# Constant products in TensorE's pauses, another split of the first list, and its tokens by pairs of groups, in a mixture-of-experts kernel on Trainium2

## The chip, the cores and the metric

The kernel runs on one core of a Trainium2 chip. The core has TensorE (matrix products, 128 by 128), VectorE and ScalarE (elementwise work), GpSimd (here constants and the issue of indirect transfers) and SyncE (issue of transfers). In the profile they are called PE (its weight loads PEld), DVE, ACT, POOL and SP. The metric is the device time of one execution in microseconds. TensorE and PSUM ([...]where products land) are what the other engines work for.

## The reference

Eight batches of 512 tokens with 512 features are scaled by a style of the batch, multiplied by one 512x512 matrix, normalised, biased and clipped (y). A router gives each of the 4096 tokens a softmax score for 8 experts. Each expert takes the 1024 tokens with its highest scores, runs a feed-forward layer of width 2048 on them, and adds its output, times the score, to the rows of those tokens.

```python
styles = cond @ (affine_w / sqrt(256)).T + affine_b
y = clip(einsum('blc,oc->blo', x * styles[:, None], weight) * dcoefs[:, None] + bias, -256, 256)
scores = softmax(y.reshape(4096, 512) @ Wr)            # 8 experts
G, idx = top_k(scores.T, 1024)                         # each expert picks its tokens
h = gelu(einsum('ekd,edh->ekh', y_tokens[idx], W1) + b1)
X = einsum('ekh,ehd->ekd', h, W2) + b2
out = x + zeros.at[idx].add(G[..., None] * X)
```

## The kernel before, in words

**Stage 1, the projection (lines 285 to 707).** Batch 0 is turned by TensorE (`turn_x0`) and multiplied by the whole matrix; batches 1 to 7 are turned by VectorE (`turn_x`) and multiplied in seven products of half-size blocks instead of eight (`unit`, with sums of blocks). `in_order` (line 366) makes each TensorE instruction that it is given follow the one given before; everything else is placed by a planner from its estimates of time. The first TensorE work is the style product, which waits for the first two transfers. Behind each batch come `score_products` and `score_softmax` (line 515): the maximum, exponentials, their sum and its reciprocal, then the scores `S` (8 per token), a copy `S0` of expert 0's score, `reps` (S0 repeated, to be turned into `R`), and `topc`, which counts for each of 64 thresholds how many of the batch's tokens reach it (an elementwise comparison `getop`, then a reduction). `store_scores` writes S behind the features in `y_dram`, where a token's row is 512 features and 8 scores.

**The first list (`route_first`, line 205).** The 1024th highest score of expert 0 is found bit by bit. `tot_top` sums the counts over partitions with a product by `ones` and fixes the top 6 bits; six rounds fix 4 bits each. In a round VectorE compares all scores with 16 candidates (`mark`, L226), TensorE adds the counts (`tot`, L229), VectorE chooses (L234, L237). Then the ranks of the chosen tokens come from two products (`rank0`, L245 and L247) and some twelve small VectorE operations: each token's place in the list, split into `lo` (place modulo 128) and `hi` (place divided by 128). In TensorE's gaps the planner puts the transposes (L703) that turn the rows of the last five batches, which ScalarE copies out and SP stores to `y_dram`.

**The list of token numbers (`indices`, line 810).** `oh` is a one-hot row of `lo` (128 columns for each of 32 token columns), `hot` one of `hi` (8 columns), `val` is `hot` times the partition number and times the column's first token. 32 small products `oh` by `val` add up to a 128x8 table of token numbers, `idx`. For expert 0 oh is made in four parts, and eight products follow each.

**Tokens (`gather`, `prepare`, lines 852 and 890).** GpSimd issues eight indirect transfers, 128 rows of `y_dram` each (groups 0 to 7). For expert 0 TensorE turns each group (L910), VectorE copies it out of PSUM (L912) into the four quarter tiles `xT[i, k]` (i: groups 0 to 3 or 4 to 7; k: half of the features), ScalarE copies out the gain (L907). When all have come, `left_sums` (L883 to L886) makes s1 to s4 on whole tiles. A transfer that copies x into out is issued by GpSimd behind the eighth gather. For the other experts the tokens take another way, through a second table in memory and VectorE's transposes.

**Stage 2, the experts.** For each expert and each half of the width there are four `hidden_unit`s and four `out_unit`s. A unit is seven block products p1, p2, p6, p7, p5, p3, p4, each two accumulating products of 128x128 by 512 (hidden). p1 and p2 need the tokens' quarters 11 and 12, p6 needs s2, p7 s3, p5 s1, p3 s4. p1, p6, p5 and p3 share the bank `a`, and ScalarE takes a snapshot (`snap`, L971) between them. `in_turns` lets the last two products of a unit overlap the next unit. The lists of the seven other experts (`route_others`, with `mark` at L736 on VectorE and `tot_b` at L726 on TensorE) are worked out during the first hidden units.

Of the kernel before, what the change touches and what calls it, by code (L numbers as in the profile page):

```python
# [11 lines left out]
F32 = mybir.dt.float32  # L12
# [13 lines left out]
def tile_modulated_expert_choice_ffn(  # L26
# [26 lines left out]
    GH = HALF // P  # L53
    GAIN = 1.0 / math.sqrt(W)
# [18 lines left out]

    ident = const.tile([P, P], F32, name="ident")
# [3 lines left out]
    ones = const.tile([P, P], BF16, name="ones")  # L78
    nc.gpsimd.memset(ones, 1.0)
# [22 lines left out]
    iota_hi = const.tile([P, KG], BF16, name="iota_hi")  # L102
    nc.gpsimd.iota(iota_hi, pattern=[[1, KG]], base=0, channel_multiplier=0,
# [15 lines left out]
    NR = (30 - TOP) // RB  # L119
    M = 1 << RB  # L120
# [84 lines left out]
    def route_first(p1c, reps, topc):  # L205
# [6 lines left out]
        for n in range(B):  # L212
            nc.tensor.matmul(tot, ones, topc[:, n, :], start=(n == 0), stop=(n == B - 1))
# [6 lines left out]
        for n in range(NR):  # L220
            cand = rt2.tile([P, 1], I32, tag="cand0", name=f"cand0_{n}")
            nc.vector.tensor_scalar(cand, owns[:, n : n + 1], thr[:, 0:1].bitcast(I32), None,
                                    op0=ALU.bitwise_or)
            mark = p1c.tile([P, ST_G, P], BF16, tag="mark0", name=f"mark0_{n}")
            cnt = rt2.tile([P, 1], F32, tag="cnt0", name=f"cnt0_{n}")
            nc.vector.tensor_scalar(mark, R, cand.bitcast(F32), None, op0=ALU.is_ge, op1=ALU.add,  # L226
                                    accum_out=cnt)
            ps = ps_small.tile([P, M], F32, tag="small", name=f"tot0_{n}")
            nc.tensor.matmul(ps, cnt.to_broadcast([P, P]), of, start=True, stop=True)  # L229
            cands = rt2.tile([P, M], I32, tag="cands0", name=f"cands0_{n}")  # L230
            nc.vector.tensor_scalar(cands, digits[:, n, :], thr[:, 0:1].bitcast(I32), None,
                                    op0=ALU.bitwise_or)
            ok = rt2.tile([P, M], F32, tag="ok0", name=f"ok0_{n}")
            nc.vector.scalar_tensor_tensor(ok, ps, float(K), cands.bitcast(F32),  # L234
                                           op0=ALU.is_ge, op1=ALU.mult)
            thr = rt2.tile([P, 1], F32, tag="thr0", name=f"thr0_{n}")
            nc.vector.tensor_reduce(thr, ok, AX.X, ALU.max)  # L237
# [7 lines left out]
        nc.tensor.matmul(ps[:, 0, :, :].rearrange("p a t -> p (a t)"), ones, flat,  # L245
                         start=True, stop=True)
        nc.tensor.matmul(ps[:, 1, :, :].rearrange("p a t -> p (a t)"), upper, flat,  # L247
                         start=True, stop=True)
# [23 lines left out]
        nc.vector.tensor_scalar(part, pos_i, P - 1, None, op0=ALU.bitwise_and)  # L272
# [3 lines left out]
        nc.vector.tensor_scalar(part2, pos_i, 7, None, op0=ALU.logical_shift_right)  # L276
# [13 lines left out]
    with tc.tile_pool(name="p1c", bufs=1) as p1c, tc.tile_pool(name="p1", bufs=2) as p1, \  # L290
# [72 lines left out]

        behind = {}

        def in_order(make, engine="PE"):

            if engine in behind:
                with tc.issue_after(behind[engine].ins):
                    behind[engine] = make()  # L370
            else:
                behind[engine] = make()
            return behind[engine]
# [141 lines left out]
        def score_softmax(b, ps):  # L515
# [15 lines left out]
            nc.vector.tensor_tensor(S[:, here, :], ex,  # L531
                                    sm.unsqueeze(2).to_broadcast([P, LT, E]), ALU.mult)
            nc.vector.tensor_copy(S0[:, here], S[:, here, 0])
# [3 lines left out]
            nc.vector.tensor_tensor(ge, S0[:, here].unsqueeze(1).to_broadcast([P, 1 << TOP, LT]),  # L537
                                    top.bitcast(F32).unsqueeze(2).to_broadcast([P, 1 << TOP, LT]),
                                    ALU.is_ge)
# [152 lines left out]
        score_softmax(B - 1, lg)  # L692
# [3 lines left out]
        places = {0: route_first(p1c, reps, topc)}  # L696
# [113 lines left out]
    def indices(e):  # L810
# [7 lines left out]
            iota_hi.unsqueeze(1).to_broadcast([P, NT, KG]), ALU.is_equal,  # L818
# [6 lines left out]

        parts = 1 if e else 4
        for n in range(parts):
            here = slice(n * NT // parts, (n + 1) * NT // parts)
            nc.vector.tensor_tensor(  # L829
                oh[:, here, :], lo[:, here].unsqueeze(2).to_broadcast([P, NT // parts, P]),  # L830
                iota_lo.unsqueeze(1).to_broadcast([P, NT // parts, P]), ALU.is_equal,
            )
# [7 lines left out]
        nc.vector.tensor_copy(idx[:, e, :], idx_f)  # L840

# [10 lines left out]
    def gather(e, i):  # L852

        z = gp.tile([P, GH * YW], F32, tag="xg", name=f"xg_{e}_{i}")
        if e:
            rows = dram.tile([HALF, YW], F32, name=f"rows_{e}_{i}")
            z = z[:, 0 : GH * D].rearrange("p (t c) -> p t c", c=P)
        else:  # L860
            z = z.rearrange("p (g w) -> p g w", w=YW)
        for j in range(GH):
            g = i * GH + j
            to = gp.tile([P, YW], F32, tag="row", name=f"row_{e}_{g}", bufs=4) if e else z[:, j, :]
            sent = nc.gpsimd.indirect_dma_start(
                out=to[:, :], out_offset=None, in_=y_dram[:, :],
                in_offset=bass.IndirectOffsetOnAxis(ap=idx[:, e, g : g + 1], axis=0),
            )
            if e:
                nc.sync.dma_start(rows[j * P : (j + 1) * P, :], to)  # L870
        if e:
            for q in range(4):
                nc.sync.dma_start(z[q * TB : (q + 1) * TB, :, :],
                                  rows[:, q * P : (q + 1) * P].rearrange("(t a) c -> a t c", a=TB))
            with nc.allow_non_contiguous_dma(reason="512 values"):
                nc.sync.dma_start(gains[e][:, i * GH : (i + 1) * GH],
                                  rows[:, D + e : D + e + 1].rearrange("(g p) o -> p (g o)", p=P))
        gathered[e, i] = z
        return sent
# [9 lines left out]

    def prepare(e):  # L890

        xT = {}
        for i in range(2):
            for k in range(2):
                xT[i, k] = fx.tile([P, 2, HALF], F32, tag=f"xT{i}{k}", name=f"xT{i}{k}_{e}")
        gain = gains.pop(e)
        ngain = fx.tile([P, KG], F32, tag="ngain", name=f"ngain_{e}")
        for i in range(2):
            xg = gathered.pop((e, i))
            for k in range(2):  # L900
                if e:
                    nc.vector.transpose(
                        xT[i, k].rearrange("p j (t b) -> p t j b", b=TB),
                        xg[:, :, 2 * k * TB : 2 * (k + 1) * TB].rearrange("p t (j a) -> p t j a", a=TB))
            for j in range(0 if e else GH):
                g = i * GH + j
                nc.scalar.copy(gain[:, g : g + 1], xg[:, j, D + e : D + e + 1])  # L907
                ps = ps_t.tile([P, DC, P], F32, tag="t", name=f"ps_xg{e}_{g}")
                for dc in range(DC):
                    nc.tensor.transpose(ps[:, dc, :], xg[:, j, dc * P : (dc + 1) * P], ident)  # L910
                for k in range(2):
                    nc.vector.tensor_copy(xT[i, k][:, :, j * P : (j + 1) * P],  # L912
                                          ps[:, 2 * k : 2 * k + 2, :])
        nc.vector.tensor_scalar_mul(ngain, gain, -1.0)
        s = {n: fx.tile([P, 2, HALF], F32, tag=f"x{n}", name=f"x{n}_{e}")
             for n in ("s1", "s2", "s3", "s4")}
        left_sums(xT[0, 0], xT[0, 1], xT[1, 0], xT[1, 1], s)
        s["11"], s["12"], s["22"] = xT[0, 0], xT[0, 1], xT[1, 1]
        tokens[e] = s, gain, ngain
# [35 lines left out]

    def hidden_unit(e, p, u, H):

        s, _, _ = tokens[e]
# [6 lines left out]
        def mm(ps, left, right, start):  # L965
            product(ps, [blk[right][:, k, u * P : (u + 1) * P] for k in range(2)],
                    [s[left][:, k, :] for k in range(2)], start)

# [5 lines left out]
        def p1():  # L974
            st["a"] = bank("a", name, 2)
            mm(st["a"], "11", (0, 0), True)
            st["s1"] = snap(1)

        def p2():
            st["b"] = bank("b", name, 1)  # L980
            mm(st["b"], "12", (1, 0), True)
# [27 lines left out]
        return [p1, p2, p6, p7, p5, p3, p4]  # L1009
# [88 lines left out]
    def fetch(e):  # L1098
# [3 lines left out]
        for i in range(2):  # L1102
            sent = gather(e, i)
        return sent
# [5 lines left out]

    with tc.issue_after(fetch(0).ins):
        nc.gpsimd.dma_start(out.rearrange("b l d -> b (l d)").rearrange("b (r w) -> (b r) w", r=16),
                            x.rearrange("b l d -> b (l d)").rearrange("b (r w) -> (b r) w", r=16))
    prepare(0)
    for e in range(E):
        b2_sb = fx.tile([P, D], F32, tag="b2", name=f"b2_{e}")
        nc.sync.dma_start(b2_sb, b2[e, :].partition_broadcast(P))
        for p in range(NP):
            nxt = (e, p + 1) if p + 1 < NP else (e + 1, 0)
            H = fx.tile([P, U, 2, KG * P], F32, tag="H", name=f"H_{e}_{p}")  # L1120
# [5 lines left out]
            in_turns([partial(hidden_unit, e, p, u, H) for u in range(U)], work)  # L1126
# [48 lines left out]
```

## Time and profile before

| what | value |
|---|---|
| median of three runs | 1750.04 us (1749.76 to 1750.58) |
| the profiled execution | 1749.67 us, span from first to last instruction 1747.9 us |
| TensorE busy | 1708.3 us, 98% |
| VectorE, ScalarE, GpSimd busy | 835.7, 478.3, 292.2 us |
| chain that ended last | TensorE 87%, VectorE 2% |
| mean granted clock of TensorE | 0.992 |

In the profile a line of an order of time gives start and duration in us, the engine, the line of the kernel, the operation, the tile written, the tiles read, the shape, the type and how many records, and in square brackets how long the engine was idle before and what ended that. An f32 product shows as two records, a transpose as one. A line of a table of stages gives the stage, its length, then busy us and instruction counts of PE, PEld, DVE, ACT and POOL, the granted clock of TensorE, the busy share of the DMA engines and GB/s. Times of a line come from the one profiled execution.

### The profile page before, as it was taken

Reading aid. Unit: us, or ns where it says so; the run is one execution under the profiler, and the core shown is the slowest. Engines: PE = TensorE matmul, PEld = TensorE weight load, DVE = VectorE, ACT = ScalarE, POOL = GpSimd, SP = SyncE. Lnnn points to the kernel's source line nnn. Section 1 sums busy time; section 2 is a strip of 40 time slices with the busy share of each in tenths; the row PEclk is TensorE's granted clock in tenths of the full one; section 3 lists DMA queues with packets and bytes.
Section 4 is the critical chain, followed back from the end, with each engine's and each line's share of the span. In section 5 each row is a group of like instructions: output and inputs, shape, how many; then the busy total and the mean of one; then the engine's idle time right before and its main releaser. Section 6 shows DMA issues by size and latency. Waiting matters only on the chain.

```text
span 1747.9 us, 17152 instructions
## 1 busy us (share of the span) xinstructions
PE 1708.3 (98%) x6522; PEld 1128.9 (65%) x6522; DVE 835.7 (48%) x1465; ACT 478.3 (27%) x842; POOL 292.2 (17%) x238
## 2 busy tenths in 40 slices
PE   8995999999999999999999999999999999999997
PEld 4774475665748485666748485766758484756656
DVE  5885883624536254524535254614445254614341
ACT  3543312223131322223231313222231313222231
POOL 0112013020222013020312013110312012110202
PEclk9997999999999999999999999999999999999999
DMA  9625627541573227441574237442574137332403
GB/s 205 172 50 177 211 49 165 121 90 48 96 201 67 54 52 173 109 84 50 98 197 79 48 64 179 89 80 55 108 184 88 45 66 182 79 79 61 84 0 49
DMA packets 143250, 178.57 MB, mean 102 GB/s; under 512 B 16824, under 2 KB 92856, under 8 KB 143040
## 3 DMA queue, kind: packets, MB, share of 16 engines
q1 hardware_dynamic: 118240, 115.19, 24.5%
q0 software_dynamic: 24912, 62.27, 21.1%
q8 instruction: 51, 0.84, 0.2%
q14 instruction: 31, 0.25, 0.1%
q10 hardware_dynamic: 16, 0.02, 0.0%
HBM read 120.46 MB, written 65.37 MB: 106 GB/s over the span
## 4 chain that ended last, share of the span: by engine, by line
PE 87%; DVE 2%; issue 0%; DMA 0%; POOLq 0%; POOL 0%; DVEq 0%
PE ps_a_o L953 25%; PE ps_a_h L953 25%; PE ps_c_o L953 12%; PE ps_c_h L953 12%; PE ps_b_h L953 6%; PE ps_b_o L953 6%; DVE mark L736 0%; PE ps_idx L835 0%; DVE oh L829 0%; DMA xg<-y_dram,idx 0%; PE ps_xg L910 0%; DVE ps_b_h L982 0%; POOLq L1171 0%; DVE hs_o L884 0%; DVE hs_o L883 0%
## 5 line engine op out<-in xcount | busy, mean ns | idle before, releaser
L1065 POOL DMA_INDIRECT out<-o_o,idx x128 | 212.3, 1659 | 1248.8 <-DVE o_o L1062 553.2
L953 PE MATMUL ps_a_o<-w_t,hs_o 128*128 128x256 f32 x1024 | 243.6, 380 | 1.2
L953 PE MATMUL ps_a_h<-xs,w_t 128*128 128x512 f32 x512 | 241.1, 593 | 0.0
L953 PEld LDWEIGHTS ps_a_o<-w_t,hs_o 128*128 128x128 f32 x1024 | 192.3, 190 | 33.4 <-issue 7.0
L971 ACT COPY snap_h<-ps_a_h 128x512 f32<-128x512 f32 x192 | 111.7, 582 | 236.9 <-PE ps_a_h L953 231.8
L953 PEld LDWEIGHTS ps_a_h<-xs,w_t 128*128 128x128 f32 x512 | 97.0, 190 | 123.0 <-issue 122.1
L1032 ACT ACTIVATE snap_o<-ps_a_o,gain 128x256 f32<-128x256 f32 x128 | 60.6, 474 | 347.5 <-PE ps_a_o L953 347.5
L997 DVE TENSOR_TENSOR snap_h<-snap_h,ps_c_h 128x512 f32<-128x512 f32 x64 | 43.9, 686 | 217.5 <-ACT snap_h L971 217.5
L982 DVE TENSOR_TENSOR ps_b_h<-ps_b_h,snap_h 128x512 f32<-128x512 f32 x64 | 44.7, 699 | 202.9 <-PE ps_b_h L953 202.9
L953 PE MATMUL ps_a_h<-xT,w 128*128 128x512 f32 x256 | 125.6, 598 | 0.0
L953 PE MATMUL ps_a_o<-w,H 128*128 128x256 f32 x512 | 124.1, 379 | 0.0
L953 PE MATMUL ps_c_o<-w,hs_o 128*128 128x256 f32 x512 | 123.8, 379 | 0.0
L953 PE MATMUL ps_a_h<-xs,w 128*128 128x512 f32 x256 | 122.0, 599 | 0.0
L953 PE MATMUL ps_a_o<-w,hs_o 128*128 128x256 f32 x512 | 121.5, 380 | 0.0
L953 PE MATMUL ps_b_o<-w,H 128*128 128x256 f32 x512 | 121.2, 379 | 0.0
L953 PE MATMUL ps_b_h<-xT,w 128*128 128x512 f32 x256 | 120.8, 593 | 0.0
L953 PE MATMUL ps_c_h<-xs,w 128*128 128x512 f32 x256 | 120.5, 593 | 0.0
L953 PE MATMUL ps_c_h<-xT,w_t 128*128 128x512 f32 x256 | 120.5, 593 | 0.0
L953 PE MATMUL ps_c_o<-w_t,H 128*128 128x256 f32 x504 | 119.1, 379 | 0.0
L953 PEld LDWEIGHTS ps_a_o<-w,H 128*128 128x128 f32 x512 | 97.1, 190 | 27.0 <-issue 15.5
L953 PEld LDWEIGHTS ps_a_o<-w,hs_o 128*128 128x128 f32 x512 | 96.0, 190 | 21.4 <-ACT snap_o L1032 8.9
L953 PEld LDWEIGHTS ps_c_o<-w,hs_o 128*128 128x128 f32 x512 | 97.1, 190 | 14.0 <-issue 0.6
(248 smaller groups left out, 1935.9 us busy)
## 6 DMA issues: line engine op xcount, KB each, us to landing
w<-in_w SPq DMA_DIRECT2D x120, 512.0 KB, 4.0
rows<-row SPq DMA_DIRECT2D x56, 260.0 KB, 4.0
xg<-rows SPq DMA_DIRECT2D x56, 256.0 KB, 6.6
x<-in_x SPq DMA_DIRECT2D x28, 256.0 KB, 8.8
y_dram<-ytok SPq DMA_DIRECT2D x5, 1024.0 KB, 4.4
w<-in_w SPq DMA_DIRECT2D x32, 128.0 KB, 4.1
y_dram<-ytok POOLq DMA_DIRECT2D x12, 256.0 KB, 4.8
b<-in_b SPq DMA_DIRECT2D x8, 256.0 KB, 4.0
```

The costliest lines, as they stand in the source:

```text
L953: nc.tensor.matmul(ps, lefts[k], rights[k], start=(start and k == 0), stop=(k == n - 1), skip_group_check=True)
L971: nc.scalar.copy(t, st["a"])
L982: added = nc.vector.tensor_add(st["b"], st["b"], st["s1"])
L997: nc.vector.tensor_add(st["u4"], st["u4"], st["c"])
L1032: nc.scalar.mul(t, st["a"], scale)
L1065: nc.gpsimd.indirect_dma_start(out=last_rows[g] if e == E - 1 else out_rows, out_offset=bass.IndirectOffsetOnAxis(ap=idx[:, e, g : g + 1], ...
```

## The change

`ones` is made first. `idle(n, ps)` issues n constant bf16 products of 128x128 by 512 (ones by ones) into a PSUM tile that nobody reads, each in order behind the TensorE instruction given to `in_order` before. There are nine at the very start, four after the count of each of the last two rounds, eight after the rank products, and sixteen after the products of the first list.

In the last batch S0 is made from the exponentials and the reciprocal directly, S comes after `getop`, and the reduction into `topc` is left out: `tot_top` adds the four slices of `getop` by four products.

The place in the first list is split into 64 low and 16 high values: `oh` has 64 columns, `hot` 16. One half of `val` is made by ScalarE. Each token column has two products, for the two halves of the partitions of the table. hot, val and oh lie in the two buffers that hold the gathered tokens afterwards.

The gathers come in pairs (group j of each half). After the transposes of a pair, VectorE copies the first half's group and ScalarE the second's, `left_sums` works on that pair's 128 columns, and units 0 and 1 multiply their p1 and p2 for these columns (`begin`); the second unit's bank b is taken from the ring of c. The gains are copied in two operations behind all tokens. For the other experts the code is moved, with the same instructions.

```diff
+    IDLE0, IDLE1, IDLE2 = 9, 8, 16
...
+    def idle(n, ps):
+        for _ in range(n):
+            in_order(partial(nc.tensor.matmul, ps.rearrange("p (a k) -> p a k", k=P), ones,
+                             ones.unsqueeze(1).to_broadcast([P, HALF // P, P]), start=True, stop=True))
+
+    ones = const.tile([P, P], BF16, name="ones")
+    nc.gpsimd.memset(ones, 1.0)
+    idle(IDLE0, ps_mm.tile([P, HALF], F32, tag="c", name="ps_idle0", bufs=2))
...
+    LO, HI = P // 2, 2 * KG
...
-        for n in range(B):
-            nc.tensor.matmul(tot, ones, topc[:, n, :], start=(n == 0), stop=(n == B - 1))
+        for n in range(B - 1):
+            nc.tensor.matmul(tot, ones, topc[:, n, :], start=(n == 0), stop=False)
+        for t in range(LT):
+            nc.tensor.matmul(tot, ones, last_top[:, :, t], start=False, stop=(t == LT - 1))
...
+            if n > NR - 3:
+                idle(4, ps_mm.tile([P, HALF], F32, tag="a", name=f"ps_idle_{n}", bufs=2))
...
+        idle(IDLE1, ps_mm.tile([P, HALF], F32, tag="b", name="ps_idle1"))
...
-        nc.vector.tensor_scalar(part, pos_i, P - 1, None, op0=ALU.bitwise_and)
+        nc.vector.tensor_scalar(part, pos_i, LO - 1, None, op0=ALU.bitwise_and)
...
-            nc.vector.tensor_tensor(S[:, here, :], ex,
-                                    sm.unsqueeze(2).to_broadcast([P, LT, E]), ALU.mult)
-            nc.vector.tensor_copy(S0[:, here], S[:, here, 0])
+            last = b == B - 1
+            if not last:
+                scores()
+            nc.vector.tensor_mul(S0[:, here], ex[:, :, 0], sm)
...
+            if last:
+                with tc.issue_after(done.ins):
+                    scores()
+                return ge
...
+    def first_indices():
+        lo, hi = places[0]
...
+        nc.vector.tensor_tensor(hot, hi.unsqueeze(2).to_broadcast([P, NT, HI]),
+                                iota_hi.unsqueeze(1).to_broadcast([P, NT, HI]), ALU.is_equal)
...
+        nc.scalar.mul(val[:, :, 0, :], hot, iota_p[:, 0:1])
+        nc.vector.tensor_tensor(val[:, :, 1, :], hot,
+                                iota_t.unsqueeze(2).to_broadcast([P, NT, HI]), ALU.mult)
+        parts = 4
+        ps = ps_small.tile([P, 2, KG], F32, tag="small", name="ps_idx0")
+        for n in range(parts):
+            here = slice(n * NT // parts, (n + 1) * NT // parts)
+            nc.vector.tensor_tensor(
+                oh[:, here, :], lo[:, here].unsqueeze(2).to_broadcast([P, NT // parts, LO]),
+                iota_lo[:, 0:LO].unsqueeze(1).to_broadcast([P, NT // parts, LO]), ALU.is_equal)
+            for t in range(NT)[here]:
+                for q in range(P // LO):
+                    in_order(partial(
+                        nc.tensor.matmul, ps[q * LO : (q + 1) * LO, :, :], oh[:, t, :],
+                        val[:, t, :, :].rearrange("p a (g q) -> p q a g", q=P // LO)[:, q, :, :],
+                        start=(t == 0), stop=(t == NT - 1), skip_group_check=True))
+        idle(IDLE2, ps_mm.tile([P, HALF], F32, tag="b", name="ps_idle2"))
...
+    def first_tokens(started):
...
+        for j in range(GH):
+            for i in range(2):
+                g = i * GH + j
+                sent = nc.gpsimd.indirect_dma_start(
+                    out=half[i][:, j, :], out_offset=None, in_=y_dram[:, :],
+                    in_offset=bass.IndirectOffsetOnAxis(ap=idx[:, 0, g : g + 1], axis=0))
...
+        for j in range(GH):
+            cols = slice(j * P, (j + 1) * P)
+            for i in range(2):
+                ps = ps_t.tile([P, DC, P], F32, tag="t", name=f"ps_xg_{i}_{j}")
+                for dc in range(DC):
+                    in_order(partial(nc.tensor.transpose, ps[:, dc, :],
+                                     half[i][:, j, dc * P : (dc + 1) * P], ident))
+                for k in range(2):
+                    if i:
+                        copied = nc.scalar.copy(xT[i, k][:, :, cols], ps[:, 2 * k : 2 * k + 2, :])
+                    else:
+                        nc.vector.tensor_copy(xT[i, k][:, :, cols], ps[:, 2 * k : 2 * k + 2, :])
+            left_sums(*[xT[i, k][:, :, cols] for i in range(2) for k in range(2)],
+                      {n: t[:, :, cols] for n, t in s.items()})
+            for f in started:
+                f(cols)
+        for i in range(2):
+            with tc.issue_after(copied.ins):
+                nc.scalar.copy(gain[:, i * GH : (i + 1) * GH], half[i][:, :, D])
...
+        def begin(cols):
+            s = tokens[e][0]
+
+            for to, left, right in (("a", "11", (0, 0)), ("b", "12", (1, 0))):
+                if to not in st:
+                    st[to] = bank("c" if u and to == "b" else to, f"{name}_{to}", 1 if to == "b" and not u else 2)
+                for k in range(2):
+                    in_order(partial(nc.tensor.matmul, st[to][:, cols],
+                                     blk[right][:, k, u * P : (u + 1) * P], s[left][:, k, cols],
+                                     start=(cols.start == k == 0), stop=(k == 1),
+                                     skip_group_check=True))
...
+    first_indices()
+    gains[0] = fx.tile([P, KG], F32, tag="gain", name="gain_0", bufs=2)
+    H = fx.tile([P, U, 2, KG * P], F32, tag="H", name="H_0_0")
+    early = [hidden_unit(0, 0, u, H, early=True) for u in range(2)]
+    first_tokens([begin for begin, _ in early])
```

## Prediction

> **What bounds the kernel now.** I read the page first (engine totals, then the forty slices), then busy time by stage, then the order of time around the two places where TensorE isn't full, and last what TensorE waits for afterwards.
>
> ```profile
> PE 1708.3 (98%) x6522; PEld 1128.9 (65%) x6522; DVE 835.7 (48%) x1465; ACT 478.3 (27%) x842; POOL 292.2 (17%) x238
> ...
> PE   8995999999999999999999999999999999999997
> ...
> PEclk9997999999999999999999999999999999999999
> ```
>
> TensorE is the bound: 98% busy, and the chain that ended last is 87% TensorE. Only the first slice and the fourth (131 to 175 us) are thin, and there the clock row dips too. In stages of 4 us (sum of TensorE, loads, VectorE, ScalarE, GpSimd busy; then granted clock, DMA share, GB/s):
>
> ```profile
> 142.00:146.00 4.00, 3.58 (x28) 2.85 (x28) 2.67 (x13) 3.06 (x6) 0.00 (x0) 1.00 1.00 359
> ...
> 150.00:154.00 4.00, 0.61 (x4) 0.41 (x4) 2.89 (x15) 0.21 (x1) 0.00 (x0) 1.00 1.01 375
> 154.00:158.00 4.00, 0.28 (x8) 0.28 (x8) 3.83 (x14) 0.00 (x0) 0.00 (x0) 0.51 0.19 65
> ...
> 170.00:174.00 4.00, 3.62 (x14) 2.36 (x13) 2.29 (x7) 0.57 (x3) 3.06 (x4) 0.50 0.77 211
> 174.00:178.00 4.00, 4.00 (x19) 2.33 (x18) 2.49 (x9) 1.76 (x4) 0.00 (x0) 0.93 1.31 492
> ```
>
> From 150 to 166 us TensorE waits for the first expert's list and its tokens; at 154.1 us its clock halves and comes back at 174.6. The same stretch in order of time:
>
> ```profile
> 155.45 0.43 DVE L816 TENSOR_TENSOR hot<-hi,iota_hi 128x256 bf16<-128x256 bf16 x1
> ...
> 156.45 4.62 DVE L829 TENSOR_TENSOR oh<-lo,iota_lo 128x1024 bf16<-128x1024 bf16 x4
> ...
> 161.76 0.17 DVE L840 CAST idx<-idx_f 128x8 int32<-128x8 f32 x1
> 163.16 1.04 POOL L865 DMA_INDIRECT xg<-y_dram,idx  x1 [23.88 <-issue]
> ...
> 166.65 1.12 PE L910 MATMUL ps_xg<-ident,xg 128*128 128x128 f32 x4 [5.14 <-DMA xg<-y_dram,idx]
> ...
> 173.03 1.80 PE L953 MATMUL ps_a_h<-xT,w 128*128 128x512 f32 x2
> ...
> 175.81 0.19 ACT L907 COPY gain<-xg 128x1 f32<-128x1 f32 x1 [1.00 <-DMA xg<-y_dram,idx]
> ```
>
> Read it as a chain: one-hot rows on VectorE (5.6 us), the index, 1.2 us to the first gather, 3.5 us to the first transpose, a gather each 1.25 us, the eighth landed by 175.81. From then on TensorE pauses for nothing that matters: the waits listed between 177 and 245 us sum to 1.3 us, and stages of 97 us after 274 us hold 96.5 to 96.9 of it.
>
> So every microsecond is measured as **when the unbroken TensorE work begins**. Before: the last transposes start at 176.40 and take 0.6 us, to 177.0; of expert products, 4 records of 0.43 us (1.72 us, the first product of unit 0) are done by then. Equivalent start 177.0 - 1.72 = **175.3**.
>
> **The start.** Nine constant products from about 1.0 us, ahead of TensorE's first real one:
>
> ```profile
> 4.98 1.87 PE L372 MATMUL ps_style<-aff_sb,cond_sb 128*8 128x512 f32 x2 [4.98 <-DMA cond_sb<-in_condT]
> ...
> 8.48 1.98 PE L370 MATMUL ps_x<-ident,x 128*128 128x128 f32 x8
> ...
> 12.20 0.72 PE L370 MATMUL ps_x<-ident,x 128*128 128x128 f32 x4 [1.16 <-DVE xmT L370]
> ```
>
> The clock row says 1.00 here, but the durations don't: the four style records take 0.83 us each where a 512-column record later takes 0.43. No row has a bf16 product of 512 columns; [...]the f32 record of 0.43 bounds the warm one from above. [...]Warm, style ends at 6.7 instead of 8.5. The second half of the first x lands at 2.24 + 5.8 = 8.05 us; the remaining 6 of 8 transposes at 0.11 (five take 0.74 warm) end at about 9.0, the four small style transposes (0.41 warm, 0.64 here) at 9.4 instead of 11.04. Gain **1.6**; 0.6 if the clock had come up earlier before or comes up later after. From 12.2 to 31.5 us TensorE is continuous, x_1 and the weights land some 4 us ahead of need, so it carries through to the scores at 134 us.
>
> **Last batch.** S0 comes straight from ex and sm: one operation of 0.19 us (0.22 with its gap) leaves the path, and the reduction of getop (0.42) becomes three more TensorE products of 64 columns (some 0.05 each). Gain 0.6 less 0.1: **0.5** (0.2 if they queue behind late transposes). The displaced score product comes back behind getop; its store has over 15 us to the first gather. [...]the late transposes they push end at 149.4 and their store lands at 154, five us before a gather even when moved up: **0**, at worst -0.2 where the second four touch the rank products. The eight behind the ranks lie in a VectorE stretch of 4.6 us: 0.
>
> **First list.** oh halves (32x64), hot and val double. A bf16 operation of 256 elements takes 0.42 us and of 1024 1.22, so 512 take 0.69, and 0.61 from one to the next (1024: 1.135 pitch). On VectorE hot, one val and four oh: 6 x 0.61 = 3.66 against 5.61 (155.45 to 161.06); the other val is on ScalarE, idle since 150 us, beside the second. Gain 1.95. TensorE now has 16 small products per part instead of 8; at the 0.034 us of the 32-column score products (32 in 1.08) a part takes 0.54, below VectorE's 0.61, and the tail after the last part grows by 0.3. Net **1.6**; 0.5 if each costs 0.053 and TensorE paces the parts.[...]
>
> So tokens come 3.7 us earlier: first transpose 163.0, second landing 164.45, eighth 172.1.
>
> **Tokens by pairs.** Per pair TensorE does eight transposes (0.88), and 16 records of 128 columns for units 0 and 1. Copies are split, VectorE 0.76 (L912, two) and ScalarE about as much; left sums are 4 x 0.41 on quarter tiles (L763, a 128x256 operation): VectorE 2.4 us per pair, below TensorE's time. The first product needs only group j of the first half: it starts 1.1 us after the pair's first transpose (0.44, 0.2 out of the array, a 0.38 copy). What a 128-column record costs is the open number p. Its multiply is 0.107 (a quarter of 0.43). Its weight load:
>
> ```profile
> 151.44 0.30 PEld L229 LDWEIGHTS tot<-of,cnt 128*128 128x128 f32 x2 [1.62 <-DVE mark L226]
> ...
> 1710.69 1.70 PEld L953 LDWEIGHTS ps_a_o<-w,H 128*128 128x128 f32 x8
> 1710.90 1.89 PE L953 MATMUL ps_a_o<-w,H 128*128 128x256 f32 x8
> ```
>
> Two loads in 0.30, of 0.19 each: one per 0.11. [...]eight full-array products of 256 columns go by at 0.216 each, their bare multiply, with eight loads inside. I take **p = 0.112**[...].
>
> First product at 165.0 (164.45, 0.44 of transposes, 0.1 for the handover); a pair takes 1.1 + 16p = 2.89 (gathers: one pair per 2.5, so TensorE paces). Last early product ends 165.0 + 3 x 2.89 + 1.79 = 175.5; s2 for p6 about 0.2 later (ScalarE copies, then three sums): 175.7. ScalarE's copies now wait for transposes, and the gains and unit 0's first snap are queued behind them: 1.85 + 0.38 + 0.59 us after the last pair's first transpose, 2.8, while p6, which overwrites what the snap reads, comes at 3.1: no stall. GpSimd issues the same eight gathers in another order and the copy of x to out behind the last, as before; no transfer on SP moves. By 175.7, 16 records of 0.43 (6.9 us) of hidden work are done: equivalent start 168.8, **6.5 us before 175.3**. Off that I take 0.7: VectorE is 18.3 of 20 us busy in 197 to 237 with the other experts' lists, whose counts TensorE waits for; 6.9 us of TensorE work leave that stretch and only 4.9 us of left sums do. Gain 5.8. Profiled execution 1749.67 (span 1747.9) to 1743.9; the median lies 0.37 above it: **1744.2**.
>
> **The clock among the tokens.** [...]The row: from 138 to 150 us TensorE does almost only transposes, and the granted clock stays 1.00. I follow the row.
>
> **Rivals.** (a) The forecast, gain 4.5 to 7.5: 0.66; more than that, with idle gaps also filled later: 0.03. (b) A head part doesn't come through (x or the clock sets the start, TensorE paces the index, or more waits on VectorE's counts): gain 2.5 to 4.5, near 1746.5. For it: 0.92 of VectorE in use; against: the start is plainly cold. 0.17. (c) Loads not hidden, or the clock falls: p of 0.15 to 0.26, gain between 3.5 and -3.5, about 1749: 0.09. (d) Slower: load and multiply fully in series, with the whole 0.187 of a load, p = 0.294, in these 64 records: start 168.3 + 64p + 0.2 - 6.9 + 0.7 = 181.1, 5.8 us after 175.3, time 1755.9. It decides from p = 0.20 (no gain) and passes the bound at 0.26. 0.05.
>
> 0.2% (3.5 us) is about what a measurement can tell from no change. Faster: (a) 0.69 and half of (b), 0.78; same: half of (b) and (c), 0.17; slower 0.05. Range: gain 1.6 to 7.5, so 1742.5 to 1748.5, which leaves out the top of (a) and most of (c) and (d).
>
> **What would show it.** Style records near 0.43 us and the ninth idle product before 4.95; first gather near 159.5; clock 1.00 from 150 to 180; 16 early records in 1.8 us per pair; the p6 products of unit 0 near 175.7. Wrong if the early records take over 0.2, the clock row dips after 155, or waits on L736 grow beyond 2 us.

## The result and the profile after

The changed kernel takes 1745.70 us (median of 13 executions, 1744.94 to 1747.78), the kernel before beside it 1749.76 (13 executions, 1748.92 to 1750.85). The ratio is 0.9977, 95% interval 0.9969 to 0.9984: a gain of 4.1 us, small but clear of the noise, since the interval leaves out 1. The forecast was 1744.2 us with a range of 1742.5 to 1748.5. The profiled execution took 1745.7 us (span 1743.9, which is 4.0 less than before).

The page of the changed kernel, with the rows for TensorE's total and its two rows of forty slices:

```profile
PE 1718.0 (99%) x6646; PEld 1136.2 (65%) x6646; DVE 830.8 (48%) x1467; ACT 480.2 (28%) x845; POOL 293.5 (17%) x238
...
PE   9998999999999999999999999999999999999997
...
PEclk9999999999999999999999999999999999999999
```

The fourth slice is now 80% full or more, and at this grain the clock row has no dip left. TensorE's busy sum grew by 9.7 us, since the 41 constant products are counted in it; it says nothing of the gain.

The start, from the order of time of the changed kernel (start, duration, engine, line, operation, tiles, shape, count, idle time before):

```profile
1.41 3.62 PE L81 MATMUL ps_idle<-ones 128*128 128x512 bf16 x8
...
4.96 2.62 PE L81 MATMUL ps_style<-aff_sb,cond_sb 128*8 128x512 f32 x4
...
7.51 1.52 PE L81 MATMUL ps_x<-ident,x 128*128 128x128 f32 x8
...
8.96 0.64 PE L81 MATMUL ps_styleT<-ident,style_rows 8*128 8x8 f32 x4
```

The constant products end at 5.03 us, as the first operands land. The clock comes up inside the style product (four records in 2.62 us, 3.57 before), the eight transposes behind it take 1.52 us instead of 1.98, and from the small style transposes on everything is 1.44 us earlier, up to the first projection product of batch 1 (tile ps_ya), here before and after:

```profile
31.57 1.03 PE L370 MATMUL ps_ya<-xmT,wt_sb 128*128 128x256 f32 x4
```

```profile
30.13 1.03 PE L81 MATMUL ps_ya<-xmT,wt_sb 128*128 128x256 f32 x4
```

That row is called **the start** below.

The stages, from the table of the changed kernel (busy us and counts of PE, PEld, DVE, ACT, POOL; granted clock; DMA share; GB/s):

```profile
150.00:154.00 4.00, 2.84 (x15) 0.95 (x12) 2.89 (x17) 0.00 (x0) 0.00 (x0) 1.00 0.72 262
154.00:158.00 4.00, 0.24 (x10) 0.28 (x12) 2.24 (x4) 0.72 (x1) 0.00 (x0) 0.83 0.18 60
158.00:162.00 4.00, 4.00 (x67) 2.51 (x64) 1.81 (x5) 0.00 (x0) 0.14 (x1) 0.50 0.04 14
162.00:166.00 4.00, 3.95 (x16) 1.60 (x14) 0.02 (x1) 0.00 (x0) 3.09 (x4) 0.81 0.47 124
166.00:170.00 4.00, 3.11 (x27) 2.96 (x28) 2.46 (x7) 0.68 (x2) 3.08 (x4) 1.00 0.74 208
```

The clock still halves, but from 156.6 to 163.5 us (0.83 of one stage and 0.81 of another) instead of 154.1 to 174.6, and no expert product lies in it. Real work fills TensorE from 167 us on.

The first list and the first tokens, from the order of time of the changed kernel:

```profile
147.94 1.02 PE L81 MATMUL ps_idle<-ones 128*128 128x512 bf16 x4
...
148.80 0.38 PE L727 MATMUL ps_yt<-ident,yT 128*128 128x128 f32 x2
...
149.83 0.36 SPq L731 DMA_DIRECT2D y_dram<-ytok  x1
...
153.44 0.17 DVE L303 CAST hi<-part 128x32 bf16<-128x32 int32 x1
155.76 0.69 DVE L868 TENSOR_TENSOR hot<-hi,iota_hi 128x512 bf16<-128x512 bf16 x1 [2.15 <-DMA y_dram<-ytok]
...
157.76 2.35 PE L81 MATMUL ps_idx<-oh 128*64 128x16 bf16 x64 [4.89 <-DVE oh L874]
...
160.36 0.17 DVE L892 CAST idx<-idx_f 128x8 int32<-128x8 f32 x1
...
161.86 1.04 POOL L966 DMA_INDIRECT xg<-y_dram,idx  x1 [23.50 <-issue]
```

Here is the line that the prediction did not have: VectorE, with `hi` ready, stands idle for **2.15 us until the last store of token rows has landed**, before it may write `hot`. The list itself is short, as forecast: from `hot` to the end of `idx` 4.8 us, before 6.5. But from `hi` to the first gather it is 8.42 us, before 7.92 (163.16 less the start of this row of the kernel before):

```profile
155.24 0.17 DVE L278 CAST hi<-part 128x32 bf16<-128x32 int32 x1
```

And the tokens by pairs, from the same view:

```profile
167.38 0.61 PE L81 MATMUL ps_a_h_a<-xT,w 128*128 128x128 f32 x4
167.83 0.61 PE L81 MATMUL ps_b_h_b<-xT,w 128*128 128x128 f32 x4
...
175.18 1.04 PE L81 MATMUL ps_xg<-ident,xg 128*128 128x128 f32 x8
176.29 0.71 PE L81 MATMUL ps_a_h_a<-xT,w 128*128 128x128 f32 x4
...
178.18 1.88 PE L1028 MATMUL ps_a_h_a<-xs,w_t 128*128 128x512 f32 x4
```

Four early records go by in 0.45 us, 0.112 each. p6 of unit 0 starts at 178.18 with 6.88 us of hidden products done (16 records of 0.43), an equivalent start of **171.3 us**, 4.0 before 175.3. The span is shorter by the same 4.0, so the whole gain is made by here, and what follows gives nothing back.

### The profile page after: what moved, and what is told of

It is laid out like the page before. It is cut to its first block, busy times and chain, and to the rows that moved or that the text cites. A ratio compares the mean times of both kernels' runs of the same rounds, so it can differ in the third digit from the quotient of the medians.

```text
span 1743.9 us, 17415 instructions
## 1 busy us (share of the span) xinstructions
PE 1718.0 (99%) x6646; PEld 1136.2 (65%) x6646; DVE 830.8 (48%) x1467; ACT 480.2 (28%) x845; POOL 293.5 (17%) x238
## 4 chain that ended last, share of the span: by engine, by line
PE 93%; DVE 4%; ACT 1%; issue 1%; DMA 1%; POOL 0%; POOLq 0%; DVEq 0%; ACTq 0%
PE ps_a_o L1028 25%; PE ps_a_h L1028 23%; PE ps_c_o L1028 12%; PE ps_c_h L1028 12%; PE ps_b_o L1028 6%; PE ps_b_h L1028 6%; PE ps_ya L81 2%; PE ps_yc L81 1%; DVE oh L849 1%; PE ps_y L81 1%; ACT xmT L500 1%; DVE mark L760 1%; PE ps_yt L727 1%; PE ps_a_h_a L1028 0%; PE ps_yb L81 0%
## 5 line engine op out<-in xcount | busy, mean ns | idle before, releaser
L1028 PE MATMUL ps_a_h<-xs,w_t 128*128 128x512 f32 x496 | 233.4, 592 | 0.0
L1059 ACT COPY snap_h<-ps_a_h 128x512 f32<-128x512 f32 x186 | 108.2, 582 | 230.0 <-PE ps_a_h L1028 227.0
L1028 PE MATMUL ps_a_h<-xT,w 128*128 128x512 f32 x248 | 120.7, 594 | 0.0
L1028 PE MATMUL ps_a_h<-xs,w 128*128 128x512 f32 x248 | 118.2, 599 | 0.0
L1028 PE MATMUL ps_b_h<-xT,w 128*128 128x512 f32 x248 | 116.8, 593 | 0.0
```

The lines of the kernel that those rows point to most:

```text
L1028: nc.tensor.matmul(ps, lefts[k], rights[k], start=(start and k == 0), stop=(k == n - 1), skip_group_check=True)
L1059: nc.scalar.copy(t, st["a"])
```

## The experiments

Twelve runs were made (e9 is the changed kernel again): e1 to e4, e5 to e8 and e9 to e12, each group on a chip of its own, beside the kernel before on the same chip (1750.21, 1749.94 and 1749.74 us). "Start" is ps_ya's first row, "list" the time from the start of `hi` to the first gather, "rest" the span less the start; these three are of the one profiled execution. The rest takes the start's luck out of a comparison, but it is of one execution each: for the changed kernel it was 1713.8 in one and 1715.2 in the other.

| run | median us (executions) | ratio to before, 95% | start | list | rest |
|---|---|---|---|---|---|
| before | see above | 1 | 31.57 | 7.92 | 1716.3 |
| after | 1745.70 (13) | 0.9977 [0.9969, 0.9984] | 30.13 | 8.42 | 1713.8 |
| e1 apart | 1744.31 (5) | 0.9966 [0.9952, 0.9979] | 31.32 | 6.13 | 1711.8 |
| e2 no constant products | 1747.65 (21) | 0.9986 [0.9979, 0.9992] | 30.96 | 6.68 | 1713.6 |
| e3 nine at the start only | 1745.64 (7) | 0.9975 [0.9963, 0.9986] | 30.02 | 6.62 | 1713.0 |
| e4 no early products | 1754.27 (11) | 1.0024 [1.0015, 1.0033] | 30.06 | 8.53 | 1722.3 |
| e5 old split | 1751.82 (21) | 1.0010 [1.0003, 1.0016] | 31.82 | 8.82 | 1719.0 |
| e6 before, nine at the start | 1749.64 (13) | 0.9999 [0.9990, 1.0007] | 30.53 | 7.92 | 1716.6 |
| e7 apart, nine at the start only | 1745.90 (19) | 0.9980 [0.9973, 0.9987] | 29.61 | 6.22 | 1713.7 |
| e8 no early, constants instead | 1751.85 (21) | 1.0009 [1.0002, 1.0015] | 31.89 | 8.42 | 1718.7 |
| e9 after again | 1745.83 (21) | 0.9980 [0.9973, 0.9986] | 32.74 | 9.18 | 1715.2 |
| e10 apart again | 1743.13 (7) | 0.9969 [0.9957, 0.9980] | 29.95 | 6.20 | 1711.4 |
| e11 apart, pause filled | 1743.27 (6) | 0.9966 [0.9954, 0.9978] | 29.69 | 5.96 | 1711.0 |
| e12 old split again | 1747.11 (11) | 0.9986 [0.9977, 0.9995] | 29.70 | 9.02 | 1713.9 |

The theory after the result: the list was made shorter, but its first write now waits for the stores of the last rows, because the buffer `xg` lies in memory that the pool of those rows (`p1`) gives up; before, `hot` and the two `val` operations went to other buffers, and the first to touch `xg`, at 156.45, came after the landing. The rival: the operations of the new list are slower than they look and the wait only fills time that something else would take.

**The tables apart (e1, e10).** The tables are put into three weight buffers that are free at that time.

```diff
-        hot = gp.tile([P, 2 * GH * YW], BF16, tag="xg", name="hot_0")[:, 0 : NT * HI].rearrange(
-            "p (t h) -> p t h", h=HI)
+        spare = [wpool.tile([P, 2 * U, QD], BF16, tag=f"w2_t{n}", name=f"spare_{n}").rearrange(
+            "p u d -> p (u d)") for n in (1, 2, 4)]
+        hot = spare[2][:, 0 : NT * HI].rearrange("p (t h) -> p t h", h=HI)
...
-        both = gp.tile([P, 2 * GH * YW], BF16, tag="xg", name="oh_0")
-        val = both[:, 0 : 2 * NT * HI].rearrange("p (t a h) -> p t a h", a=2, h=HI)
-        oh = both[:, 2 * NT * HI : 2 * NT * HI + NT * LO].rearrange("p (t m) -> p t m", m=LO)
+        val = spare[1][:, 0 : 2 * NT * HI].rearrange("p (t a h) -> p t a h", a=2, h=HI)
+        oh = spare[0].rearrange("p (t m) -> p t m", m=LO)
```

> The first list's three tables lie in memory that no late row of y used (the spare w2_t1, w2_t2, w2_t4 tiles), so the first comparison needn't wait for the last store of rows. Theory (the store costs 2.15 us on the path): the first table is made at about 153.5 us, first gather at 159.7, time 2.1 us below the changed kernel, about 1743.6. Rival (the wait hides another one right behind it, the store itself or the index products): within 0.7 us of the changed kernel, 1745.0 to 1745.7.

> The tables of the first list in buffers that no row store has to leave, all constant products kept. If the wait for the stores costs what the first such run showed: 1744.3 us, 1.4 below the changed kernel in the same call. Rival, that the first run of it was a chance of few executions: within 0.5 us of the changed kernel.

From the order of time of the second of these runs (e10):

```profile
153.25 0.17 DVE L303 CAST hi<-part 128x32 bf16<-128x32 int32 x1
153.37 0.69 DVE L880 TENSOR_TENSOR spare<-lo,iota_lo 128x512 bf16<-128x512 bf16 x1
...
158.05 0.17 DVE L892 CAST idx<-idx_f 128x8 int32<-128x8 f32 x1
159.45 1.04 POOL L966 DMA_INDIRECT xg<-y_dram,idx  x1 [21.29 <-DMA b<-in_b]
```

No wait behind `hi`, and the list takes 6.2 us instead of 8.4. The rest falls from 1713.8 to 1711.4 and 1711.8, by 2.4 and 2.0 us, about the wait of 2.15. The first run gave 1744.31, the second 1743.13, that one 2.7 us below the changed kernel on the same chip (1745.83). The rival is out: the wait was the list's own time, and without it the list gives what was forecast for it (7.92 to 6.2, 1.7; forecast 1.6). This version is the best of the case, with e11.

**The constant products out (e2), only the nine at the start kept (e3), and the same with the tables apart (e7).**

```diff
-    IDLE0, IDLE1, IDLE2 = 9, 8, 16
+    IDLE0, IDLE1, IDLE2 = 0, 0, 0
...
-            if n > NR - 3:
+            if n > NR:
```

e3 and e7 have `9, 0, 0` in place of `0, 0, 0`; e7 has the edit of e1 as well.

> All constant products left out, the rest as in the changed kernel. Theory (the clock is worth 1.4 us at the start and about 2 among the tokens): TensorE half speed from about 154 to 172 us, style records of 0.83 us, 3.3 us above the changed kernel, about 1749.0. Rival (constant products only fill pauses that cost nothing): within 1 us of the changed kernel, below 1746.7.

> The nine constant products at the start stay, the later ones (4, 4, 8 and 16) are left out. Theory: the start keeps its 1.4 us, the tokens lose about 2 us to a half clock, of which some 0.4 come back because late rows are no longer held up: about 1747.3. Rival (later ones worth nothing): 1745.7 or, without the held-up rows, 1745.3.

> The first list's tables apart from the rows of y, and the later constant products (4, 4, 8, 16) left out. Theory (the later products keep a clock worth 0.7 to 2 us, and cost nothing once no store is waited for): 0.7 to 2 us above the kernel with only the tables apart, 1745.0 to 1746.3. Rival (they are worth nothing in either place): equal to it, 1744.3.

e3 equals the changed kernel (1745.64 and 1745.70), where 1747.3 was expected. Three lines of its order of time and two stages of its table say why:

```profile
147.82 0.41 PE L727 MATMUL ps_yt<-ident,yT 128*128 128x128 f32 x2
...
148.88 0.36 SPq L731 DMA_DIRECT2D y_dram<-ytok  x1
...
153.87 0.69 DVE L868 TENSOR_TENSOR hot<-hi,iota_hi 128x512 bf16<-128x512 bf16 x1 [0.35 <-DMA y_dram<-ytok]
```

```profile
162.00:166.00 4.00, 2.14 (x9) 1.74 (x10) 0.76 (x2) 0.00 (x0) 3.09 (x4) 0.50 0.72 196
166.00:170.00 4.00, 3.92 (x30) 3.68 (x30) 2.57 (x7) 1.32 (x4) 3.08 (x5) 0.87 0.77 214
```

The clock is at half until 167.0 us, so the first pair's work runs slowly; that is the loss. But the four constant products of a counting round no longer stand ahead of the last late transposes (147.82; in the changed kernel 148.80, behind the products of 147.94), the last store is issued 0.95 us earlier and lands 1.9 us earlier, and `hot` waits 0.35 instead of 2.15. So the later constant products cost about as much by the store as they gain by the clock. The delay of the issue is only half of the cost: in the changed kernel the last store also takes longer from issue to landing, 5.8 us (6.6 in e9) against 4.9 in e2 and e3 and at most 4.7 before. The DMA engines are nearly idle when it is issued (share 0.06 from 149.8 to 150.3 us), and it ends in a thin tail (0.14 falling to 0.01 from 153.5 to 155.5); why it takes longer is not shown. e7 separates the two: with no store to wait for, leaving the later ones out costs 2.1 us of rest (1713.7 against 1711.4 and 1711.8). In the medians e7 is 4.0 us below its base and e1 and e10 5.9 and 6.6 below theirs. e2, without any, is 2.6 us below its base: of the changed kernel's 4.1 us, then, about 1.5 need the constant products. It lies 2.0 above the changed kernel, where 3.3 was expected. The profiles show less of it: the rest of e2 (1713.6) is no longer than that of the changed kernel.

**The early products out (e4), and the pauses filled with constants instead (e8).** The pairs, the split copies and the sums by quarter tiles stay; units 0 and 1 make p1 and p2 afterwards, whole.

```diff
-    early = [hidden_unit(0, 0, u, H, early=True) for u in range(2)]
-    first_tokens([begin for begin, _ in early])
+    first_tokens([])
...
-            if e == p == 0:
-                units[0:2] = [lambda unit=unit: unit for _, unit in early]
```

e8 has, besides, seven constant products behind the transposes of each of the first three pairs:

```diff
-            for f in started:
-                f(cols)
+            if j + 1 < GH:
+                idle(7, ps_mm.tile([P, HALF], F32, tag="c", name=f"ps_idle3_{j}", bufs=2))
```

> Tokens still come by pairs with sums by pairs, but units 0 and 1 start their first two products only when all tokens are there, as before. Theory (the early products fill 6.9 us of TensorE work in, at the price of a slower pace by pairs): transposes follow the gathers, the eighth pair's done at about 175.1, one product of 1.7 us in between, 2.5 us above the changed kernel, about 1748.2. Rival (the pace by pairs, 2.95 us against 2.5 of the gathers, eats most of it): 1746.2 to 1746.7.

> No early products of units 0 and 1, but seven constant products behind the transposes of each of the first three pairs. Theory (without the early products half of the loss was the clock, which fell at 170 us in the pauses between transposes): clock 1.00 from 166 us on, unit 0 starts at about 175.6 at full speed, time about 1750, some 4 us below the kernel without early products. Rival (the early products' fill alone is the loss): 1754.

Both missed on the slow side, e4 by 6 us and e8 by 2. The stages of e4, and its first expert product in order of time:

```profile
166.00:170.00 4.00, 1.45 (x9) 1.04 (x10) 2.68 (x8) 0.68 (x2) 3.09 (x4) 0.93 0.73 205
170.00:174.00 4.00, 2.89 (x12) 2.09 (x11) 2.34 (x7) 0.98 (x4) 2.20 (x3) 0.50 0.96 270
174.00:178.00 4.00, 2.76 (x11) 1.99 (x12) 3.04 (x9) 1.15 (x6) 0.00 (x0) 0.50 1.11 434
```

```profile
177.92 3.62 PE L1028 MATMUL ps_a_h<-xT,w 128*128 128x512 f32 x4
```

And in e8:

```profile
166.00:170.00 4.00, 2.70 (x16) 1.41 (x15) 0.92 (x3) 0.57 (x2) 2.87 (x3) 1.00 0.72 198
170.00:174.00 4.00, 3.83 (x23) 2.20 (x21) 2.12 (x7) 0.52 (x3) 3.33 (x4) 1.00 0.74 210
```

```profile
178.11 1.96 PE L1028 MATMUL ps_a_h<-xT,w 128*128 128x512 f32 x4 [0.73 <-issue]
```

Warm at 166, TensorE of e4 is busy for 1.45 of the next 4 us, with transposes alone; at about 169.4 the clock halves, transposes then take 0.24 us instead of 0.11, and the first expert product runs at half speed (3.62 us for four records). e8 holds the clock at 1.00 from 166 us on, and its first product takes 1.96. By the rest, e4 is 8.5 us above the changed kernel and e8 4.9 (7.1 and 3.5 against its second profile, e9). By the medians against their bases (+4.1, +1.9, and -4.1 for the changed kernel) it is 8.1 and 6.0. **So the early products are worth 7 to 8.5 us: 2.1 to 3.6 because they keep the clock up, 3.5 to 6 because they fill the pauses with work.** This is the largest part of the change.

**The old split (e5, and e12 once more).** 128 low and 8 high values, tables as before, the rest as changed.

```diff
-    LO, HI = P // 2, 2 * KG
+    LO, HI = P, KG
...
-    first_indices()
+    indices(0)
```

> The changed kernel with the first list by 128 low and 8 high values as before (four parts of 1024 elements), all else kept. Theory (the new list's shorter work is eaten by the wait for the last store, because its first table lies where rows of y lay; the old list's small tables don't, its large one does): the large table starts at about 155.7 us when the store has landed, the index is 0.5 us later than in the changed kernel, time about 1746.3. Rival (the split is worth its 1.6 us): 1747.3 or above.

> The 128 by 8 split in the changed kernel once more, for the pause of 3.7 us between the second pair's transposes and its copies. If it is an accident of one execution: no such pause in this profile, and about 1747 us for its execution. If it belongs to this order of work: the copies of a pair again begin together some 3 us after its transposes, and 1751.8 us.

e5 came out 5.5 us above what was expected. Its trace shows a stall that no other run has, from the order of time:

```profile
171.24 1.20 PE L81 MATMUL ps_xg<-ident,xg 128*128 128x128 f32 x8
...
175.40 0.76 DVE L995 COPY xT<-ps_xg 128x256 f32<-128x256 f32 x2 [3.66 <-remote]
175.45 0.65 ACT L993 COPY xT<-ps_xg 128x256 f32<-128x256 f32 x2 [5.04 <-remote]
175.87 0.93 PEld L81 LDWEIGHTS ps_a_h_a<-xT,w 128*128 128x128 f32 x4 [3.68 <-DVE xT L995]
```

VectorE and ScalarE both begin to copy the second pair 3 us after its transposes, released by something the trace doesn't name, and TensorE stands still for 3.4 us. In e12, the same kernel on another chip, the second pair's transposes start at 169.16, and VectorE copies at once:

```profile
169.79 0.76 DVE L995 COPY xT<-ps_xg 128x256 f32<-128x256 f32 x2
```

No stall, then, and 1747.11 us, so it doesn't belong to this order of work. But all 21 executions of e5 were long (1749.1 to 1754.27), so it was hardly an accident of one execution either. What caused it stays open. With e12 the split's worth can be read: its rest is 1713.9, against 1713.8 and 1715.2 of the changed kernel and 1711.4 to 1711.8 with the tables apart. **As changed, the new split gained nothing in the traces**; the medians on one chip, 1747.11 and 1745.83, allow it 1.3 us. With the tables apart it is worth 2.1 to 2.5 us by the rest (4.0 by the medians of e12 and e10). The old split waits for the stores too, at its first `oh`, but only 1.01 us, since `hot` and `val` are made meanwhile.

**The start alone (e6), the changed kernel again (e9), and the pause at 9 us filled (e11).** e6 is the kernel before with the nine products only.

```diff
+    idle(9, ps_mm.tile([P, HALF], F32, tag="c", name="ps_idle0", bufs=2))
```

e11 is the tables apart, with

```diff
         turn_style(0)
+        idle(5, ps_mm.tile([P, HALF], F32, tag="b", name="ps_idle3"))
```

> The kernel before with the nine constant products at the start and nothing else. Theory (cold start costs 1.4 to 2.0 us, and nothing later takes it back): 1.4 to 2.0 us below the kernel before, about 1748.4. Rival (the first x or a later transfer sets the pace): within 0.6 us of the kernel before.

> The changed kernel unaltered, beside the next three on one chip. Both theories: 1745.7 us (1745 to 1747.8), the first row operation of the list waiting about 2 us for the store of the last rows.

> As the tables apart, with five more constant products behind the style's small transposes, in the pause of 1.2 us before 10.6 us. Theory, that this pause lets the clock fall again in some executions and so makes the start worth 1.6 us in some and nothing in others: eight projection products at 11 us all at 0.43 us each, the executions closer together, and a median 0.5 to 1 us below the tables apart, 1743.5. Rival, that the fall has nothing to do with the pause: the median of the tables apart, 1744.3, and the same spread.

e6 has the start at 30.53 in its profile, 1.04 earlier, and its median is 1749.64 to 1749.94 of its base: nothing to measure, at 13 executions from 1747.58 to 1752.57 (5.0 us wide; the 36 of the kernel before beside e9 to e12 lie between 1748.5 and 1752.7, all but one below 1750.9). e9 shows where the width is from. Its start, in order of time, and one stage:

```profile
8.97 0.98 PE L81 MATMUL ps_x<-ident,x 128*128 128x128 f32 x6 [0.72 <-DMA x<-in_x]
...
12.40 5.13 PE L81 MATMUL ps_y<-xmT,wa_sb 128*128 128x512 f32 x8
```

```profile
12.00:16.00 4.00, 4.00 (x9) 1.94 (x8) 2.25 (x4) 0.00 (x0) 0.00 (x0) 0.57 1.21 184
```

In this execution the second half of x landed at 8.97 (in the changed kernel's first profile it held TensorE up by 0.2 us at 8.04), and the clock fell again, so that eight ps_y records took 5.13 us instead of 3.60. The start is at 32.74, later than before the change. The same fall is in e1, e5 and e8 (clock 0.64 to 0.72 from 12 to 16 us). Over the eleven profiled executions with these nine products, and nothing else in that stretch, the start is 30.7 on average (29.6 to 32.7); without them it was 31.57 and, in e2, 30.96. The seven whose clock held average 30.0, the four where it fell 31.9. **By these two and eleven profiles the start is worth 0.3 to 0.9 us on average, not 1.4.** e11's profile shows no fall, its median is that of e10, and six executions lie within 2.2 us (seven of e10 within 3.4). The median speaks for the rival; the trace agrees with the theory, but seven of the eleven without the filling show no fall either. Whether the filled pause prevents the fall stays open.

## Why the prediction was right, and where it was wrong

The forecast was 5.8 us of gain; the profiled executions show 4.0 and the medians 4.1. That is inside the stated range, but not inside the forecast's own case (a), a gain of 4.5 to 7.5: it is case (b), "a head part doesn't come through", to which 0.17 was given; and in the profiled execution the part that failed is none of the three that (b) names. By its own steps:

- **The start**, forecast 1.6: 1.44 in the profile shown. The mechanism was right: the nine constant products go from 1.01 to 5.03 us, and the style product behind them starts at 4.96 (4.98 before). That they would not delay it was the author's estimate. Later, at a granted clock of 1.00, four take 1.02 us and eight 1.89, which is 0.22 for each one more. The last x transpose ends at 9.03 (forecast 9.0). By the lengths of its records the clock came up within the style product, at about 6.5 us, so a style record took 0.65 us on average and not 0.43; and the small style transposes take 0.64 us here as before, not the 0.41 of the later ones (at 22.29 us). And it is not a fixed gain: the rival "x or the clock sets the start" is true in four of eleven profiled executions, and the average is below 1.
- **The last batch**, forecast 0.5: 0.48 by `ok_top` (107.76 us behind the start, before 108.24), of which the counting rounds gave 0.12 back: the time from the start to `hi` fell from 123.67 to 123.31, 0.36. This is read from the two profiles; no run leaves it out.
- **The constant products in the last two rounds, forecast 0. This is the step that failed.** It said that "their store lands at 154, five us before a gather": it looked for the first reader of the rows, a gather, and not for who next takes the memory that the rows leave. The store was issued at 149.83 and landed at about 155.7, later than forecast too, and the first table operation of the list was behind it. Price: 2.15 us of wait, 1.8 of it brought by the constant products (e3 waits 0.35). Had the tables lain elsewhere, the late store would have cost nothing (e1, e10).
- **The list**, forecast 1.6: its operations gave 1.7 (from `hot` to `idx_f` 6.10 before, 4.39 after; 64 small products in 2.35 us, 0.037 each, forecast 0.034). With the wait it is 0.5 us longer than before. So the first gather came at 161.86, not 159.5.
- **Tokens by pairs**, forecast 2.8 (6.5 less the 3.7 by which tokens come earlier): 2.7 (first gather to equivalent start 12.1 before, 9.4 after). p was 0.112, as taken from the row of the 256-column products: 16 records in 1.79 us. A pair took 2.90 to 3.01 instead of 2.89; in the longer ones the weight loads wait 0.3 for VectorE's copy.
- **The clock among the tokens**: forecast 1.00 from 150 to 180, which failed: it was 0.50 from 158 to 162. The products behind the ranks end at 152.86, TensorE is empty for 4.9 us until the list's products, and in that time, at 156.6, the clock halves. That cost nothing here: the sixteen constants behind the list took 5.31 us and ended at 165.28, just as the first tokens came; that they would fit was the author's estimate. The forecast rested on the stretch from 138 to 150 us of the kernel before, where dense transposes (TensorE busy for 3.6 to 3.7 of every 4 us) left the clock at 1.00. e4 shows that this row doesn't carry over to transposes with pauses: there the clock fell. Whether the pauses or the transposes did it, no run tells apart.
- **More waits on VectorE's counts**, forecast -0.7: none. TensorE waits for `mark` 1.1 us in five places between 177 and 245 us, no more than before.

The sum of what was measured is 1.44 + 0.36 - 0.5 + 2.7 = 4.0. That the number fell into the range is in part luck, the work of two errors that partly cancel: -2.1 for the store, +0.7 for the wait that did not come. The early products stand in the forecast only as 6.9 us of work done early; they are worth more than anything else in the change (7 to 8.5 us with the clock), because the pairs without them are slower than the kernel before (e4).

## What to carry to other kernels

When a table is put into a buffer that "is free", ask whose memory it was: here its first write waited 2.15 us for the last transfer out of it, and work pushed a microsecond later elsewhere (constant products ahead of a transpose, with the store issued 0.95 us later) moved that transfer. A constant product can have a price even in a pause, if anything later on its engine feeds such a transfer: here 1.8 us of that wait (e3 waits 0.35). If real work can fill the pause, it brings the clock and the work (2.1 to 3.6 and 3.5 to 6 us here), where constants brought the clock alone (1.00 from 166 us on in e8). Judge a gain at the start of a kernel over many executions and by the rest of the span, since one profile of it can be off by 3 us (starts from 29.6 to 32.7 us here).

## What was not expected of the hardware

The clock that nine constant products had raised at 4.0 to 6.6 us (by the lengths of the records) fell again at 10.9 to 12.1 us in four of eleven profiled executions and stayed down for 3.4 us. This is worked out from the clock of the stages from 8 to 12 and from 12 to 16 us (0.86 and 0.72 in e1 and e8, 0.93 and 0.64 in e5, 1.00 and 0.57 in e9), with 0.50 as the low clock. Eight records took 4.8 to 5.3 us there instead of 3.6. In the other seven it held, though TensorE pauses for 1.2 us before its transposes of 10.3 to 11.2 us there too.

What tells the four from the seven is not shown. TensorE's busy time from 8 to 12 us doesn't: 2.84, 2.80, 2.55 and 2.12 us in e1, e5, e8 and e9, where the clock fell, and 2.81 and 2.84 in the changed kernel and e10, where it held. In e11 the clock came up at 4.1 us, as in e1 and e8 (4.0), which both fell; with the pause filled TensorE was busy for all 4 us from 8 to 12, and the clock held, in its one profile. The other low stretches, worked out in the same way, last 6.9 us in the changed kernel, 17.0 in e3 and 20.5 before.

In e4, with pauses between the transposes and TensorE busy for 1.45 us of the stage from 166 to 170, the clock went to half within this stage (0.93 in it, 0.50 in the next); dense transposes, TensorE busy for 3.58 to 3.74 of every 4 us, had left it at 1.00 from 138 to 150 us in the kernel before. And the granted clock in the stages says 1.00 at the very start, while the style records of the kernel before take 0.83 us there, where a record of the same size later takes 0.43: at the start the row can't be read.
